# Layer A of a hybrid block: sums of weights packed four to a product, reciprocals sent round by DRAM, last rows in another order

## The chip, the cores and the metric

The kernel runs on one core of one Trainium2 chip. The metric is the time of one execution on the device, in microseconds. TensorE (PE) multiplies matrices into PSUM; VectorE (DVE), ScalarE (ACT) and GpSimd (POOL) work on tiles in SBUF, the first two on PSUM as well; SyncE (SP) issues nearly all DMAs.

## The reference

Four sequences of 2048 rows of 512 numbers go through four stages, each `x = x + f(layernorm(x))`: causal linear attention ("layer A"), a feed-forward product with both sides quantized to 8 bits, a gated recurrent attention ("layer B"), and the same feed-forward product again. The change lies in layer A and in the feed-forward product that directly follows it. Layer A is:

```python
q = relu(split_heads(x @ Wq)) + EPS          # 16 heads of 64
k = relu(split_heads(x @ Wk)) + EPS
v = split_heads(x @ Wv)
k_cumsum = cumsum(k, axis=2)                 # over the rows
context  = cumsum(einsum('bhnd,bhne->bhnde', k, v), axis=2)
D_inv = 1.0 / einsum('bhnd,bhnd->bhn', k_cumsum, q)
attn = einsum('bhnd,bhnde,bhn->bhne', q, context, D_inv)
return attn.reshape(b, n, H * DH) @ Wo + bo
```

`D_inv` is one number for each row and head: one over the sum of the weights with which earlier rows enter. The feed-forward product scales each row by its largest absolute value over 127, rounds it, does the same with the columns of `rhs`, multiplies and scales back.

## The kernel before

A flag computed from the decays chooses a code path at the start; with these inputs the "mild" one runs, `layer_a_mild` and then `layer_b_mild`. What follows is `layer_a_mild`.

The 8192 rows are cut into 16 blocks of `TA` = 512 rows. Tiles hold features on the 128 partitions and the 512 rows along the free axis, so that a pair of heads (2 x 64 features) fills the partitions; there are `NP` = 8 pairs. The main loop runs over blocks `n` and, within a block, over the pairs `hp`. One pass of the inner loop is called a slot here. In a slot `attend(B, hp)` gives six steps for one pair, and `fill` is a list of single products (one matmul each) of other work; `spread` puts the fill evenly between the six steps. The steps are

- `keys` (L815): `k` transposed on TensorE (`pkr`), copied by ScalarE to `kr`; VectorE makes the running sum of `k` within chunks of 128 rows (`qc`, a scan, L824), the carried sums (`ksum`), and multiplies by `q` (L831). `qc` has one buffer.
- `scores` (L836): eight products `pss`, masked by VectorE into `sm` (L849).
- `update` (L854): eight products `pu`, copied by ScalarE; GpSimd adds them up into `within`, the state at each chunk's start (L869).
- `weigh` (L874): the sums of weights. The product `pd` of `qc` with a matrix `same` of 128 x 128, ones in two diagonal blocks of 64, adds up the 64 features of each head and puts the sum on all 64 partitions of that head. ScalarE makes `guess` = exp(-ln(`pd`)), and VectorE `miss` = -`pd` x `guess`.
- `outputs` (L886): four products `pn` from the states and eight from `sm`. VectorE multiplies `pn` by `guess` (L906) and by 2 + `miss` (L910), one Newton step of the reciprocal, into `oT[hp]`, which has 12 buffers.
- an empty step.

The fill holds the `k` and `q` features of the next pair (`pk`, `pq`, four matmuls each), in the first four slots `values` for the second half of the heads (`pv`) and `project` for the previous block (`po`, eight matmuls over the eight `oT`), in the last four slots `values` of the next block and `pf`, the feed-forward product of a row group of the previous block. All matmuls of the helper `product` have the one line L647.

The feed-forward part for 128 rows: `ffn_levels` (L653) normalizes, finds the row's largest absolute value and rounds into `f_q`; `ffn_product` (L669) has SyncE transpose `f_q` by a DMA into `f_qT` (one buffer); `pf` is made a slot later, and VectorE and GpSimd put the result back into `xa` (L679, L680). When the last row group is in, the block is stored to DRAM as `mmid` (L966), from which layer B reads. After the last block the same loop runs once more with no attention in it: only `project`, `ffn_levels` and `pf` of that block.

`quantize_rhs` (L85) loads `rhs`, transposed, in one piece of 1 MB and quantizes it; it is called after the second slot of the first block.

PSUM is dealt out in banks: three for products (`mm`: `pk`, `pq`, `pv`, `po`, `pd`, `pf`), two for `pss`, one each for `pn`, `pu` and transposes. The framework that builds the program keeps the dependencies and may move an instruction past others on its engine, so the order on an engine is near the order of the text and not the same; every engine runs its own instructions in that order.

Of the kernel before, what the change touches and what calls it, by code (L numbers as in the profile page):

```python
# [13 lines left out]
ALU = mybir.AluOpType  # L14
# [31 lines left out]
def hybrid_block_kernel(ctx: ExitStack, tc: tile.TileContext, t: dict, out: bass.AP):  # L46
# [95 lines left out]
    def ffn(pool, bank, x, n):  # L142
# [4 lines left out]
        for i in range(n):  # L147
# [10 lines left out]
            qT = pool.tile([P, KC, P], BF16, name="f_qT", bufs=1)  # L158
# [494 lines left out]
    def ffn_levels(pool, x):  # L653

        mv, rs = stats(pool, x.unsqueeze(1), 1)
        sc = pool.tile([P, 2], F32, name="f_sc", bufs=4)
        xn = pool.tile([P, D], F32, name="f_xn", bufs=1)
        normalize(xn, x, mv, rs, 0)
        s1, v1 = sc[:, 0:1], sc[:, 1:2]
# [9 lines left out]
    def ffn_product(pool, bank, x, q, s1):  # L669

        qT = pool.tile([P, KC, P], BF16, name="f_qT", bufs=1)
# [10 lines left out]
        return [product]  # L682

    def layer_a_mild():
        with ExitStack() as es:
# [37 lines left out]
            same = w.tile([P, P], F32, name="same")  # L723
            nc.gpsimd.memset(same, 0.0)
            for h in range(2):
                nc.gpsimd.memset(same[h * DA : (h + 1) * DA, h * DA : (h + 1) * DA], 1.0)
# [77 lines left out]
            def attend(B, hp):  # L804
# [10 lines left out]
                def keys():  # L815
# [7 lines left out]
                    A.qc = pool.tile([P, TA], F32, name="qc", bufs=1)  # L823
                    nc.vector.tensor_tensor_scan(A.qc, go, k, 0.0, ALU.mult, ALU.add)  # L824
                    sums = ksum[:, hp, :]
                    ends = A.qc.rearrange("p (i t) -> p i t", t=P)[:, :, P - 1]
# [3 lines left out]
                    for i, ch in enumerate(chunks):  # L830
                        nc.vector.scalar_tensor_tensor(  # L831
                            A.qc[:, ch], A.qc[:, ch], sums[:, i : i + 1], q[:, ch], ALU.add, ALU.mult
                        )
# [40 lines left out]
                def weigh():  # L874

                    A.pd = bank([P, TA], F32, name="pd", tag="mm")
                    nc.tensor.matmul(A.pd, same, A.qc, start=True, stop=True)  # L877
                    ln = pool.tile([P, TA], F32, name="ln", bufs=1)
                    nc.scalar.activation(ln, A.pd, AF.Ln)
                    A.guess = pool.tile([P, TA], F32, name="guess", bufs=1)  # L880
                    nc.scalar.activation(A.guess, ln, AF.Exp, scale=-1.0)

                    A.miss = ln
                    nc.vector.scalar_tensor_tensor(A.miss, A.pd, -1.0, A.guess, ALU.mult, ALU.mult)

                def outputs():  # L886
# [15 lines left out]
                    for r in heads:  # L902
# [3 lines left out]
                    nc.vector.tensor_tensor(  # L906
                        A.guess, pn.rearrange("p i t -> p (i t)"), A.guess, ALU.mult
                    )
                    B.oT[hp] = pool.tile([P, TA], F32, name="oT", bufs=12)
                    nc.vector.scalar_tensor_tensor(B.oT[hp], A.miss, 2.0, A.guess, ALU.add, ALU.mult)  # L910
# [3 lines left out]
            def block(n, x):  # L914
                B = Block()
                B.n, B.x, B.xn, B.qk, B.v, B.oT, B.mul = n, x, {}, {}, {}, {}, {}
                return B

# [8 lines left out]
            for n in range(len(at) + 1):  # L927
                more = n + 1 < len(at)
                if n < len(at) and at[n][1] == 0:
# [4 lines left out]
                for hp in range(NP):  # L934
                    fill = []
                    if n < len(at):
                        if hp + 1 < NP:
                            fill += feature(B, hp + 1, "k") + feature(B, hp + 1, "q")
                        elif more:
                            fill += feature(after, 0, "k") + feature(after, 0, "q")  # L940
                        if hp < NTA:
                            fill += values(B, 1, hp)
                        elif more:
                            fill += values(after, 0, hp - NTA)
                    if prev is not None:
                        if hp < NTA:
                            fill += project(prev, hp)
                        else:
                            i = hp - NTA
                            fill = fill + prev.mul[i]  # L950
# [4 lines left out]
                    spread(attend(B, hp) if n < len(at) else [lambda: None], fill)  # L955
# [499 lines left out]
```

## Time and profile before

| | us |
|---|---|
| runs before: median (lowest to highest of 3) | 4247.15 (4246.32 to 4254.92) |
| the profiled execution | 4246.83 |
| its span, first to last instruction | 4244.9 |
| layer A, steady part (window 200 to 2540) | 2340 |
| last rows of layer A and start of layer B (window 2540 to 2625) | 85 |

What some of the groups of instructions cost in layer A, mean of one in ns (groups by line and shape, within 100 to 2540 us):

| line, engine, what | mean ns | count in the window |
|---|---|---|
| L824 DVE scan into `qc` | 1220 | 124 |
| L849 DVE mask into `sm` | 683 | 248 |
| L884 DVE `ln` (`miss`) from `pd` | 688 | 124 |
| L906 DVE `guess` from `pn` | 686 | 124 |
| L910 DVE `oT` | 770 | 124 |
| L879 ACT table load, then Ln | 1283, 598 | 125, 124 |
| L881 ACT table load, then Exp | 1283, 630 | 124, 124 |
| L822 ACT copy of `pkr` | 585 | 124 |
| L680, L748 POOL additions of 128 x 512 | 1267, 1268 | 59, 57 |

DMAs, from issue to landing (median): `mmid` 1 MB 4.3 us, `xa` 1 MB 5.1, `xb` 512 KB 3.7, the transposes into `f_qT` 2.4, `m_causal` 64 KB 2.0; rows of 2 KB spread over 128 partitions (256 KB each): `b_out_b` 4.8, `b_ln_g` 6.7, `b_ln_b` 7.8, `a_bo` 8.1.

In the timelines below a line is: start in us, time from its start to its end, engine, line, operation, output <- inputs, the part of the array used (rows * columns), shape and type, how many records were merged; in brackets, idle time before it and what ended it. A matmul of 32-bit floats leaves two records. Matmuls are pipelined, so what one costs is the time from its start to the next one's start.

### The profile page before, as it was taken

How to read it: one execution, taken by the hardware profiler on the slowest of the kernel's cores; microseconds unless marked ns; L12 is line 12 of the kernel's file. 1: busy time of each engine (PE TensorE's matmuls, PEld its weight loads, DVE VectorE, ACT ScalarE, POOL GpSimd, SP SyncE). 2: the span in 40 equal slices, each digit the busy share in tenths (PEclk: the TensorE clock that was granted, in tenths of full speed). 3: DMA queues.
4: the chain of work that ended last, by engine and by line, in shares of the span. 5: the costliest groups of instructions: out<-in, count | busy, mean ns of one | idle time of the engine just before them, and what ended most of it. 6: DMA issues, size and time to landing. Idle time of an engine off the chain costs nothing.

```text
span 4244.9 us, 55766 instructions
## 1 busy us (share of the span) xinstructions
PE 4154.5 (98%) x22421; PEld 2350.8 (55%) x22421; DVE 2320.8 (55%) x4451; ACT 1032.6 (24%) x1737; POOL 1392.8 (33%) x2527
## 2 busy tenths in 40 slices
PE   8999999999999999999999996999999999999997
PEld 4555555555555555555555554666666666666664
DVE  4455555555555555555555455566556656565655
ACT  2322322322322222222222230212111211121111
POOL 3222222222222222222222222444444444444443
PEclk9999999999999999999999998999999999999998
DMA  3000000000000000000000003011111111111100
GB/s 122 2 3 23 26 3 23 26 3 23 25 3 23 25 3 23 25 3 23 25 3 23 16 5 123 19 31 32 33 36 36 32 31 31 31 32 32 35 18 24
DMA packets 124829, 111.96 MB, mean 26 GB/s; under 512 B 73232, under 2 KB 86416, under 8 KB 124560
## 3 DMA queue, kind: packets, MB, share of 16 engines
q1 hardware_dynamic: 123440, 106.73, 8.2%
q8 instruction: 178, 2.92, 0.3%
q10 hardware_dynamic: 1120, 1.57, 0.1%
q14 instruction: 91, 0.75, 0.1%
HBM read 57.94 MB, written 33.55 MB: 22 GB/s over the span
## 4 chain that ended last, share of the span: by engine, by line
PE 93%; DVE 3%; POOL 2%; DMA 1%; issue 1%; ACT 0%; SPq 0%; POOLq 0%; DVEq 0%; ACTq 0%
PE pr L1109 11%; PE pk L647 11%; PE pv L647 11%; PE po L647 11%; PE pq L647 11%; PE pvb L647 5%; PE py L647 5%; PE pss L843 3%; PE pn L898 3%; PE pl L1142 3%; PE pn L892 3%; PE pd L877 3%; PE ps L1201 2%; PE pf L677 2%; PE pu L859 2%; PE pyT L1240 2%
## 5 line engine op out<-in xcount | busy, mean ns | idle before, releaser
L647 PE MATMUL pk<-xnTa,a_Wk 128*128 128x512 f32 x1024 | 510.2, 611 | 0.0
L647 PE MATMUL pq<-xnTa,a_Wq 128*128 128x512 f32 x1024 | 490.6, 601 | 0.0
L647 PE MATMUL pv<-a_Wv,xnTa 128*128 128x512 f32 x1024 | 478.8, 601 | 2.9 <-ACT xnTa L140 2.9
L647 PE MATMUL po<-a_Wo_sb,oT 128*128 128x512 f32 x1024 | 465.5, 598 | 0.0
L647 PEld LDWEIGHTS pv<-a_Wv,xnTa 128*128 128x128 f32 x1024 | 190.1, 191 | 229.7 <-issue 225.7
L647 PEld LDWEIGHTS po<-a_Wo_sb,oT 128*128 128x128 f32 x1024 | 189.7, 190 | 226.1 <-issue 220.2
L647 PEld LDWEIGHTS pq<-xnTa,a_Wq 128*128 128x128 f32 x1024 | 187.6, 190 | 210.7 <-issue 205.2
L125 POOL TENSOR_SCALAR rs<-mv 128x1 f32<-128x1 f32 x320 | 80.8, 253 | 610.5 <-DVE mv L124 610.0
L824 DVE TENSOR_TENSOR_SCAN qc<-go,kT 128x512 f32<-128x512 f32 x128 | 156.2, 1220 | 200.2 <-PE pd L877 200.2
L1109 PE MATMUL pr<-xnTb,m_kT_sb 128*128 128x256 f32 x1024 | 259.4, 392 | 0.0
L1109 PE MATMUL pr<-xnTb,m_qT_sb 128*128 128x256 f32 x1024 | 253.4, 391 | 0.0
L869 POOL TENSOR_TENSOR within<-state,u 64x64 f32<-64x64 f32 x256 | 80.8, 316 | 522.9 <-ACT u L864 513.3
L647 PE MATMUL pvb<-b_vT_sb,xnTb 128*128 128x512 f32 x512 | 246.9, 606 | 0.0
L849 DVE TENSOR_TENSOR sm<-pss,causal 128x512 f32<-128x512 f32 x256 | 164.3, 683 | 128.3 <-PE pss L843 127.1
L647 PE MATMUL py<-b_oT_sb,yT 128*128 128x512 f32 x512 | 231.5, 594 | 0.0
L647 PEld LDWEIGHTS pk<-xnTa,a_Wk 128*128 128x128 f32 x1024 | 169.0, 190 | 111.3 <-issue 92.8
L1109 PEld LDWEIGHTS pr<-xnTb,m_qT_sb 128*128 128x128 f32 x1024 | 185.4, 191 | 58.0 <-issue 25.9
L1109 PEld LDWEIGHTS pr<-xnTb,m_kT_sb 128*128 128x128 f32 x1024 | 184.5, 190 | 51.1 <-issue 19.9
L822 ACT COPY kr<-pkr 128x512 f32<-128x512 f32 x128 | 74.9, 586 | 557.5 <-PE pkr L820 557.5
L126 POOL TENSOR_TENSOR rs<-rs,neg_half 128x1 f32<-128x1 f32 x320 | 192.7, 603 | 23.3
L864 ACT COPY u<-pu 128x256 f32<-128x256 f32 x128 | 47.6, 372 | 620.1 <-PE pu L859 620.1
L793 DVE TENSOR_TENSOR xa<-po,xa 128x512 f32<-128x512 f32 x64 | 44.2, 691 | 263.3 <-PE po L647 263.3
(155 smaller groups left out, 6976.8 us busy)
## 6 DMA issues: line engine op xcount, KB each, us to landing
mmid<-xa SPq DMA_DIRECT2D x16, 1024.0 KB, 4.3
out<-xb SPq DMA_DIRECT2D x32, 512.0 KB, 2.8
xa<-in_x SPq DMA_DIRECT2D x15, 1024.0 KB, 5.1
xb<-mmid SPq DMA_DIRECT2D x30, 512.0 KB, 3.7
m_cos<-in_cos SPq DMA_DIRECT2D x30, 128.0 KB, 2.4
m_sin<-in_sin SPq DMA_DIRECT2D x30, 128.0 KB, 2.4
a_Wv<-in_a_Wv SPq DMA_DIRECT2D x2, 1024.0 KB, 7.6
a_Wk<-in_a_Wk SPq DMA_DIRECT2D x4, 512.0 KB, 9.6
```

The costliest lines, as they stand in the source:

```text
L126: nc.gpsimd.tensor_tensor(rs, rs, neg_half[:, :n], ALU.pow)
L647: nc.tensor.matmul(held[0], lhs(), rhs(), start=(n == 0), stop=(n == len(pairs) - 1))
L677: nc.tensor.matmul(pf, qT[:, c, :], rq[:, c, :], start=(c == 0), stop=(c == KC - 1))
L824: nc.vector.tensor_tensor_scan(A.qc, go, k, 0.0, ALU.mult, ALU.add)
L843: nc.tensor.matmul(ps[h][:, i, :], k[r, chunks[i]], q[r, chunks[i]], start=True, stop=True)
L849: nc.vector.tensor_tensor(s, ps[h], causal.unsqueeze(1).to_broadcast([P, NTA, P]), ALU.mult)
L859: nc.tensor.matmul(pu[r, i, :], A.kr[:, i, r], v()[:, i, vh[h]], start=True, stop=True, skip_group_check=True,)
L877: nc.tensor.matmul(A.pd, same, A.qc, start=True, stop=True)
L892: nc.tensor.matmul(pn[:, i, :], A.before[i], q[:, chunks[i]], start=(i == 0), stop=False, skip_group_check=True,)
L898: nc.tensor.matmul(pn[r, i, :], v()[:, i, vh[h]], A.sm[h][:, i, :], start=False, stop=True, skip_group_check=True,)
L1109: nc.tensor.matmul(pr[:, half, :], wp[name][:, c, lo : lo + P], B.xnT[:, c, :], start=(c == 0), stop=(c == KC - 1),)
L1142: nc.tensor.matmul(pl[half * 64 : (half + 1) * 64, n, :], low[name][:, f, g, half, :], B.turned[name][f][:, half, :], start=(f == 0), stop ...
```

## The change

1. `same` becomes 128 x 32: ones from the first 64 partitions to the first 16 columns, from the other 64 to the next 16. `weigh` does nothing in three slots of four. In slots 3 and 7 it makes four products, one for each of the last four pairs, each into a quarter of the 128 partitions of one bank `pd`. Each head's sum then stands on 16 partitions. `qc` gets four buffers.
2. Ln, Exp and the Newton step run once on that bank. Partition 0 of every 16 is written to DRAM (`rec`: 8 rows of 512 numbers) and loaded back, each row spread over the 64 partitions of its head, for two pairs at a time (`wide`, one buffer, two DMAs of 256 KB); after the last slot of the last block all four pairs at once, into the place of a tile `xnTa`.
3. `outputs` no longer divides: ScalarE copies `pn` to `oT`. Four `divide` steps per set multiply `oT` in place by `wide` on VectorE; they are put into the fill of the next slot at positions 6, 7, 13 and 15, and the second load follows the second of them.
4. The weights' quantization is split into four row groups, `load_part` and `quantize_part`, after the first five slots of the first block; `bo` is added row group by row group there. `f_qT` gets a second buffer.
5. The extra pass of the loop after the last block is gone. The first four products of the first two row groups of `project` are fill of the last slot; the rest of the last block is written out in an order of its own.

```diff
-            qT = pool.tile([P, KC, P], BF16, name="f_qT", bufs=1)
+            qT = pool.tile([P, KC, P], BF16, name="f_qT", bufs=2)
...
+    def load_part(pool, c):
+        rT = pool.tile([P, D], F32, name="f_xn", bufs=1)
+        nc.sync.dma_start(rT, t["rhsT"][c * P : (c + 1) * P, :])
+        return rT
+    def quantize_part(pool, bank, c, rT):
+        part = slice(c * P, (c + 1) * P)
+        q, s1 = row_levels(pool, rT)
+        transpose_rows(bank, rq[:, :, part], q, BF16)
+        wide = rT[:, 0:P]
+        nc.vector.tensor_copy(wide, s1.to_broadcast([P, P]))
+        pw = bank([P, P], F32, name="r_pw", tag="t")
+        nc.tensor.transpose(pw, wide, ident)
+        nc.scalar.copy(rscale[:, part], pw)
...
-            same = w.tile([P, P], F32, name="same")
+            same = w.tile([P, 32], F32, name="same")
             nc.gpsimd.memset(same, 0.0)
             for h in range(2):
-                nc.gpsimd.memset(same[h * DA : (h + 1) * DA, h * DA : (h + 1) * DA], 1.0)
+                nc.gpsimd.memset(same[h * DA : (h + 1) * DA, h * 16 : (h + 1) * 16], 1.0)
...
-                    A.qc = pool.tile([P, TA], F32, name="qc", bufs=1)
+                    qc = B.qc[hp] = pool.tile([P, TA], F32, name="qc", bufs=4)
...
                 def weigh():
-                    A.pd = bank([P, TA], F32, name="pd", tag="mm")
-                    nc.tensor.matmul(A.pd, same, A.qc, start=True, stop=True)
+                    if hp % 4 != 3:
+                        return
+                    pd = bank([P, TA], F32, name="pd", tag="mm")
+                    for m in range(4):
+                        nc.tensor.matmul(
+                            pd[m * 32 : (m + 1) * 32, :], same, B.qc[hp - 3 + m],
+                            start=True, stop=True, skip_group_check=True,
+                        )
                     ln = pool.tile([P, TA], F32, name="ln", bufs=1)
...
+                    nc.vector.scalar_tensor_tensor(ln, pd, -1.0, guess, ALU.mult, ALU.mult)
+                    nc.vector.scalar_tensor_tensor(guess, ln, 2.0, guess, ALU.add, ALU.mult)
+                    rec = dram.tile([4, 2, TA], F32, name=f"rec_{B.n}_{hp}")
+                    nc.sync.dma_start(rec.rearrange("m h t -> (m h) t"), guess[0:P:16, :])
+                    if B.n + 1 == len(at) and hp == NP - 1:
+                        wide = pool.tile([P, 4, TA], F32, name="xnTa")
+                        for h, r in enumerate(heads):
+                            nc.sync.dma_start(wide[r, :, :], rec[:, h, :].partition_broadcast(DA))
+                        wides = [wide[:, 0:2, :], wide[:, 2:4, :]]
+                    else:
+                        wides = [load(rec, 0)]
+                    def divide(m):
+                        o = B.oT[hp - 3 + m]
+                        nc.vector.tensor_tensor(o, o, wides[m // 2][:, m % 2, :], ALU.mult)
+                        if m == 1 and len(wides) == 1:
+                            wides.append(load(rec, 2))
+                    weights.extend([lambda m=m: divide(m) for m in range(4)])
+                def load(rec, m):
+                    wide = pool.tile([P, 2, TA], F32, name="wide", bufs=1)
+                    for h, r in enumerate(heads):
+                        nc.sync.dma_start(wide[r, :, :], rec[m : m + 2, h, :].partition_broadcast(DA))
+                    return wide
...
-                    nc.vector.tensor_tensor(
-                        A.guess, pn.rearrange("p i t -> p (i t)"), A.guess, ALU.mult
-                    )
                     B.oT[hp] = pool.tile([P, TA], F32, name="oT", bufs=12)
-                    nc.vector.scalar_tensor_tensor(B.oT[hp], A.miss, 2.0, A.guess, ALU.add, ALU.mult)
+                    nc.scalar.copy(B.oT[hp], pn.rearrange("p i t -> p (i t)"))
...
-            for n in range(len(at) + 1):
+            for n in range(len(at)):
...
+                    if not more and hp == NP - 1:
+                        row = [project(B, i) for i in range(NTA)]
+                        fill += row[0][:4] + row[1][:4]
...
+                    for place, f in zip((6, 7, 13, 15), weights):
+                        fill.insert(place, f)
+                    weights.clear()
+                    spread(attend(B, hp), fill)
+                    if n == 0:
+                        if 1 <= hp <= NTA:
+                            quantize_part(pool, bank, hp - 1, part)
+                            nc.gpsimd.tensor_tensor(B.x[:, hp - 1, :], B.x[:, hp - 1, :], bo, ALU.add)
+                        if hp < NTA:
+                            part = load_part(pool, hp)
...
+            run(row[2][:4])
+            run(weights)
+            run(row[0][4:])
+            levels(prev, 0)
+            run(row[1][4:])
+            levels(prev, 1)
+            run(row[2][4:] + row[3][:4] + prev.mul[0])
+            levels(prev, 2)
+            run(row[3][4:] + prev.mul[1])
+            levels(prev, 3)
+            run(prev.mul[2] + prev.mul[3])
+            store(prev)
```

`row_levels` is the second half of the former `ffn_levels`, from the largest absolute value on; `levels` calls `ffn_levels` and `ffn_product` for one row group, `store` writes `mmid`.

## The prediction

> **What bounds the kernel now.** I read the page first: busy shares, then the chain that ended last.
>
> ```profile
> PE 4154.5 (98%) x22421; PEld 2350.8 (55%) x22421; DVE 2320.8 (55%) x4451; ACT 1032.6 (24%) x1737; POOL 1392.8 (33%) x2527
> ...
> PE 93%; DVE 3%; POOL 2%; DMA 1%; issue 1%; ACT 0%; SPq 0%; POOLq 0%; DVEq 0%; ACTq 0%
> PE pr L1109 11%; PE pk L647 11%; PE pv L647 11%; PE po L647 11%; PE pq L647 11%; PE pvb L647 5%; PE py L647 5%; PE pss L843 3%; PE pn L898 3%; PE pl L1142 3%; PE pn L892 3%; PE pd L877 3%; PE ps L1201 2%; PE pf L677 2%; PE pu L859 2%; PE pyT L1240 2%
> ```
>
> TensorE is 93% of the chain, and `pd`, the product that the change packs, is 3% of it. Shares are averages, so next the windows: layer A in its steady state, and its last rows with the start of layer B.
>
> ```profile
> 200.00:2540.00 2340.00, 2339.38 (x11561) 1224.65 (x11560) 1232.42 (x2295) 657.25 (x881) 579.57 (x1413) 1.00 0.05 16
> 2540.00:2625.00 85.00, 52.13 (x178) 28.44 (x178) 43.38 (x144) 6.76 (x11) 25.22 (x37) 0.78 0.48 151
> ```
>
> After span and PE come PEld, DVE, ACT, POOL, clock, DMA. In 2340 us TensorE idles 0.6 us at full clock: there a matmul taken away is time taken away, until another engine is late. Vector is at 53%. In the last rows TensorE is 39% idle; there waits count.
>
> **Removed: 128 `pd` products.** A "busy" of 593 ns overlaps its neighbours; the cost is start to next start, from the timeline.
>
> ```profile
> 1005.64 1.02 PE L877 MATMUL pd<-qc,same 128*128 128x512 f32 x2
> 1006.50 1.88 PE L647 MATMUL pv<-a_Wv,xnTa 128*128 128x512 f32 x4
> 1008.22 1.02 PE L647 MATMUL po<-a_Wo_sb,oT 128*128 128x512 f32 x2
> ```
>
> One f32 product is two records, 0.86 us from 1005.64 to 1006.50 (0.43 each). 128 x 0.86 = 110.1 us.
>
> **Added: 32 sets of four, each a quarter of the columns.** If the quarters run one after another, nothing is gained (4 x 0.86). The nearest row is layer B's `pyT`: products of 32 columns, four quarters, a different moving operand each.
>
> ```profile
> 3009.61 0.64 PE L1240 MATMUL pyT<-ab,vb 128*32 128x128 f32 x16
> 3010.18 2.86 PE L1109 MATMUL pr<-xnTb,m_qT_sb 128*128 128x256 f32 x12
> ```
>
> Sixteen records of 128 columns; at 0.43/4 = 0.107 us each they would take 1.71 us one by one. They take 0.57: four rounds of four (0.43) plus 0.14. Cut to 3009.64 to 3009.68 the timeline shows four records begun together, and no more:
>
> ```profile
> 3009.61 0.32 PE L1240 MATMUL pyT<-ab,vb 128*32 128x128 f32 x4
> ```
>
> So a set of `pd` is 2 rounds x 0.43 + 0.14 = 1.00 us; 32 sets are 32.0. Net **-78.1 us**.
>
> Two rules of the Trainium skill speak against this. "TensorE: Matmul & The Clock Gate", Part 3, says that matmuls start and end in strict program order. Both passes of a product sit on one quarter; if the second waits for the first and the next quarter may not overtake, four quarters need five rounds, 5 x 0.43 + 0.14 = 2.29 us, and the net is 110.1 - 73.3 = 36.8. The same reading would give `pyT` nine rounds, 0.96 us, where the row has 0.57: I take the row. "TensorEngine Tiling", Key Properties, says that a change of tiling mode drains the array. `pd` was whole among whole products; now each set has a drain on each side. The pipeline's tail is what a record lasts beyond its spacing, 0.593 - 0.43 = 0.16 us; two would make 1.18 us a set, 6 us more in all. But `pyT` too stands beside whole products on both sides, so its 0.14 holds the drains; 1.00 stays, 1.18 is the bad end. The good end, no overhead, is 0.86: 4.5 us better.
>
> **Evictions.** Per pair Vector loses three passes (`ln` 0.69, `guess` 0.69, `oT` 0.77) and gains a multiply by the broadcast (SBUF only, like `oT`: 0.77); per set it gains two passes. 128 x 1.38 - 32 x 1.4 = 132 us less work. Scalar trades Ln, Exp and two table loads (0.60 + 0.63 + 2 x 1.28 = 3.8 us) for a copy of 0.59, and keeps the 3.8 once a set. Both hide under TensorE, so zero. `qc` with four buffers ends Vector's wait on `pd` (200 us in the rows); off the path, zero.
>
> **The round trip through DRAM is the new wait.** In the built order the first divide is queued on Vector right behind the second reciprocal pass; behind it wait the eviction of row 3's `po`, the FFN levels, and the next slot's masked scores, for which TensorE's `pn` waits. After `pd`: Ln 0.60, table 1.28, Exp 0.63, two passes 1.4, gaps and drain 0.3: 4.2 us. The write of 16 KB: no row of its own; 64 KB land in 2.0 (`m_causal`); with issue 2.4. Two broadcasts of 256 KB: the nearest rows, one row spread over 128 partitions, landed in 4.8 (`b_out_b`), 6.7 and 7.8 us (in a crowd of 11 loads), and 512 KB of `xb` in 3.7; I take 4.8 because little else moves here (DMA share 0.05), plus 0.6 issue. Sum 12.0 us after `pd`, between 10.5 and 15.
>
> Against it, fourth slot: `pd` ended at 1051.47 and the next slot began at 1063.03, 11.6 us later. So the data land 0.4 us into the next slot, two divides end at 2.0; before, Vector began the same work at 0.2 (1063.23) and finished the scores at 6.4 (1069.40). Delayed, they finish at 8.2. `pn` took them at 1074.75, 11.7 into the slot, 10.9 without `pd`. Slack 2.7 us: hidden. The second broadcast (issued at 2.0, landed by 7.4) is ready when Vector, done with the scores at 8.2, asks. Eighth slot: the rest of the slot after `pd` is 8.0 us, data at 4.0 into the next, divides to 5.5, the `kT` eviction and scan behind it to 7.7, scores by 9; `pn` needs them at 13.4. Slack 4.4. `oT` of the last pairs is wanted by `project` only after that. SP holds the write, the broadcasts, `mmid`, `xa` and the FFN transposes in one queue; in the built order a transpose waits up to a slot behind the second broadcast, but its product comes two slots later. Zero, up to 2.3 us a fourth slot (16 of them) at the 15 us end, 37 in all.
>
> **Slots without `pd`.** It also stood between `pu` and `pn`, which waits for GpSimd's `within`. In the last slot these were ready 3.5 us after `pu` began (2537.60 to 2541.14); without `pd` there remain `pu` 0.62 + four products 3.44 + 0.7 of `pn` = 4.8. Covered; where GpSimd first finishes an addition of 1.27 us, a little is not. +3 us over the layer (0 to 8); half of it is block 0, where this wait was already 1.24 us.
>
> **The quantized weights** come in four parts after slots 2 to 5 of block 0. The same 20 transposes; each part's load and Vector's 2 us sit beside slots that have no previous block to finish. Zero (-1 to +2).
>
> **The last rows.** Before, all 32 `po` products ran first (2543.5 to 2570.9), then `pf` waited for transposes one at a time, since `f_qT` had one buffer:
>
> ```profile
> 2570.93 1.03 PE L677 MATMUL pf<-rq,f_qT 128*128 128x512 bf16 x4
> 2574.33 1.04 PE L677 MATMUL pf<-rq,f_qT 128*128 128x512 bf16 x4 [2.38 <-DMA f_qT<-f_q]
> 2581.44 1.89 PE L677 MATMUL pf<-rq,f_qT 128*128 128x512 bf16 x4 [6.07 <-DMA f_qT<-f_q]
> 2588.18 1.89 PE L677 MATMUL pf<-rq,f_qT 128*128 128x512 bf16 x4 [4.86 <-DMA f_qT<-f_q]
> ```
>
> From the last `pd` (2538.91) to the issue of `mmid` (2592.30): 53.4 us. After, from `pd`: TensorE has 1.0 + two `po` 1.7 + `pn` 2.0 + seven `po` 6.0 = 10.7 us; the divided `oT` are back at 1.0 + 12.0 + 0.8 = 13.8, so it idles 3 us. Sixteen `po` bring 27.6. Row levels take Vector about 5 us each (2550.53 to 2555.80 shows one), rows overlap with each other's `po`, a transpose 2.5; in the built order the fourth levels end near 39.5, transpose 42, `pf` at half clock 1.9, `f_y` 0.75, addition 1.27: issue at 46. Gain 7.4, less 2.7 us of work that moved ahead of `pd`. Layer B's first loads follow `mmid` as before, with `b_oT` now among them: +1. Net -4 (-8 to +2).
>
> **Sum:** -78.1 + 3 - 4 = -79 us. Profiled execution 4246.8 (span 4244.9 and 1.9 around it), so 4167.8; the median of the runs, 4247.15, is 0.3 above it: **4168**.
>
> **Rivals.**
> - *The round trip costs part of the gain* (broadcasts of 7 to 8 us, as in the crowded rows): 3 us late, up to 0.7 us a fourth slot on TensorE, and Vector later still where it works near the slot's length; 10 to 30 us back, 4178 to 4198. For: partition broadcasts are the slow rows. Against: an idle DMA. 11%.
> - *Five rounds*: -36.8 + 3 - 4: 4209. For: the order rule. Against: `pyT`. 7%.
> - *Slower: Vector's queue at the first divide.* All behind it waits. With lateness x over my 12.0, a pair of sets loses (x - 2.7) + (x - 4.4) against a gain of 2 x 2.44 + 0.25 from the tail: even at x = 6.1, a landing of 10.9 us instead of 4.8. At 14 us (x = 9.2) a pair loses 11.3 against 5.1: 16 x 6.2 = 99, 4346. For: Vector is first in, first out, and the page has no read broadcast from freshly written DRAM. Against: no 256 KB row over 8.1. 5%.
> - *The quarters don't overlap at all*: two drains and no gain, near 4250. 1%; `pyT` excludes it.
>
> Forecast 76%. By itself it spans 4155 (no overhead, tail -8) to 4184 (drains, GpSimd at 8, tail +2). With most of the first rival: 4155 to 4193. A difference under 0.2% (8.5 us) can't be told from none here. Faster 0.94, same 0.01, slower 0.05.
>
> **What would show it.** `pd`: 256 records still, start to next start near 1.0 us a set (2.3: five rounds; 3.4: none overlap). TensorE idle in steady layer A under 8 us; a wait of `pn` for Vector's `sm` in the slot after a set is the DRAM rival, and the landing of `wide` says why. `mmid`'s last issue about 46 us after the last `pd`. Layer B unchanged. I am wrong if `wide` lands past 8 us or a set costs over 1.2.

## The result, and the profile after

| | median us (lowest to highest) | ratio to before, 95% interval |
|---|---|---|
| before, 4 runs beside the change | 4248.9 (4246.32 to 4254.92) | |
| after, 4 runs | 4199.38 (4198.64 to 4200.68) | 0.9882 [0.9865, 0.9899] |

The change makes the kernel 1.2% faster. I had forecast 4168 and a range of 4155 to 4193, so the direction was right and the gain too large by two thirds: the profiled execution (4199.37) has a span of 4197.5, 47.4 us below before, where my sum said 79. The page of the changed kernel, busy shares and chain:

```profile
PE 4100.3 (98%) x22421; PEld 2308.2 (55%) x22421; DVE 2200.0 (52%) x4271; ACT 749.0 (18%) x1484; POOL 1456.5 (35%) x2527
...
PE 91%; POOL 3%; DVE 3%; DMA 1%; issue 1%; ACT 0%; SPq 0%; ACTq 0%; POOLq 0%; DVEq 0%
```

and the windows of layer A's steady part and of its last rows with the start of layer B (columns as before):

```profile
200.00:2480.00 2280.00, 2276.81 (x11523) 1179.69 (x11522) 1114.33 (x2111) 391.45 (x640) 635.94 (x1407) 1.00 0.11 30
2480.00:2580.00 100.00, 64.75 (x237) 34.78 (x235) 54.60 (x160) 11.98 (x20) 34.62 (x50) 0.78 0.43 139
```

Vector and Scalar have the relief that was forecast, and TensorE is still what the steady part consists of. But it idles 3.2 us there where it idled 0.6, and its busy time over the whole kernel fell by 54 us (4154.5 to 4100.3), not by the 78 of the products that went. The last rows with the start of layer B are about as idle as they were, 35% (39% before). Where the 32 us are, read off as the times at which the same work begins in both traces (the start of `pkr` opens a slot; `pl`, `pvb` and `pke` are among the first products of layer B, in this order):

| stretch | my sum | measured |
|---|---|---|
| start to the first slot | 0 | +1.5 |
| block 1 | -4.9 + 1.5 | -0.2 |
| blocks 2 to 15 | 14 x -4.88 + 1.4 = -66.9 | -55.05 |
| block 16 up to its last slot | -4.9 | -2.7 |
| last slot to the issue of the last `mmid` | -4.6 | -0.2 |
| from there to layer B's first `pke` | +1 | +6.2 |
| rest of layer B, last stores | 0 | +3.0 |

(The +1.5 at the start is the scatter of the first loads: in the thirteen kernels below the first slot began 0.7 to 2.4 us earlier than in this one execution.)

**What came as forecast.** The quarters overlap. A set in the changed kernel, timeline of TensorE:

```profile
1026.76 1.98 PE L647 MATMUL pq<-xnTa,a_Wq 128*128 128x512 f32 x4
1028.58 1.02 PE L647 MATMUL pv<-a_Wv,xnTa 128*128 128x512 f32 x2
1029.54 1.06 PE L901 MATMUL pd<-qc,same 128*32 128x512 f32 x8
1030.53 2.84 PE L647 MATMUL pv<-a_Wv,xnTa 128*128 128x512 f32 x6
1033.21 1.02 PE L647 MATMUL po<-a_Wo_sb,oT 128*128 128x512 f32 x2
```

From 1029.54 to 1030.53 the set costs 0.996 us; I had 1.00. But look at its neighbours. Two records of `pv` before the set take 0.96 (1028.58 to 1029.54), and two whole records are 0.86; six behind it take 2.68 and are 2.58. The set is entered and left at 0.1 us each, and this stands in the rows of the products beside it. Summed over the 28 sets of blocks 2 to 15 the excess is 0.093 before and 0.104 behind a set, 5.5 us.

The round trip is hidden, as forecast: `wide` lands 4.0 us after issue (median of 124), and TensorE's list of waits has no `pn` waiting for Vector. It has three entries that my sum lacked or had too small (columns: who waited for what, us in total, times, longest):

```profile
PE pf L680 <- DMA f_qT<-f_q: 25.8, 5, 9.4
...
PE po L647 <- DVE oT L925: 4.1, 1, 4.1
PE pn L943 <- POOL within L889: 3.5, 10, 0.8
```

### The profile page after: what moved, and what is told of

Same layout as the page of the kernel before. It is cut to its first block, busy times and chain, and to the rows that moved or that the text cites. A ratio compares the mean times of both kernels' runs of the same rounds, so it can differ in the third digit from the quotient of the medians.

```text
span 4197.5 us, 55714 instructions
## 1 busy us (share of the span) xinstructions
PE 4100.3 (98%) x22421; PEld 2308.2 (55%) x22421; DVE 2200.0 (52%) x4271; ACT 749.0 (18%) x1484; POOL 1456.5 (35%) x2527
## 3 DMA queue, kind: packets, MB, share of 16 engines
q1 hardware_dynamic: 142400, 140.81, 11.3%
## 4 chain that ended last, share of the span: by engine, by line
PE 91%; POOL 3%; DVE 3%; DMA 1%; issue 1%; ACT 0%; SPq 0%; ACTq 0%; POOLq 0%; DVEq 0%
PE pr L1184 12%; PE pk L647 11%; PE pv L647 11%; PE po L647 11%; PE pq L647 10%; PE pvb L647 5%; PE py L647 5%; PE pss L863 3%; PE pn L949 3%; PE pl L1217 3%; PE pn L943 3%; PE ps L1276 2%; PE pf L680 2%; PE pu L879 2%; PE pyT L1315 2%; PE pg L647 2%
## 5 line engine op out<-in xcount | busy, mean ns | idle before, releaser
L889 POOL TENSOR_TENSOR within<-state,u 64x64 f32<-64x64 f32 x256 | 106.4, 416 | 546.7 <-ACT u L884 537.1
L889 POOL TENSOR_TENSOR within<-within,u 64x64 f32<-64x64 f32 x512 | 208.3, 407 | 38.3
L682 DVE SCALAR_TENSOR_TENSOR f_y<-pf,f_sc,rscale 128x512 f32<-128x512 f32 x128 | 94.6, 739 | 225.9 <-PE pf L680 200.4
```

Of the source, the lines that this page charges most:

```text
L682: nc.vector.scalar_tensor_tensor(y, pf, s1, rscale, ALU.mult, ALU.mult)
L889: nc.gpsimd.tensor_tensor(A.before[i + 1][r, r], A.before[i][r, r], u[r, i, :], ALU.add)
```

## The experiments

All are the changed kernel with one thing altered unless said otherwise; four runs each, beside seven of the kernel before on the same chip. The spans and slots are those of the profiled execution. In blocks 2 to 15 the slots repeat to 0.01 us from one kernel to the next where nothing touches them, so a difference of 0.1 us can be read, with one exception: the mean of the fifth slots, which follow a set, lies between 16.66 and 16.75 in the variants that leave them alone (16.67 in the changed kernel). A span also carries the scatter of the first loads, up to 2.4 us. The readings of the last rows rest on one trace for each kernel, and the runs of one kernel lie up to 10 us apart (those of the best version).

### Twice: is the overhead the set's, or the neighbours'?

```diff
-                    for m in range(4):
+                    for m in (0, 1, 2, 3, 0, 1, 2, 3):
```

> Every set of four pd products is issued twice in a row; the result is the same. Against the changed kernel. Theory (the cost that I missed is the change of tiling on the way into and out of a set, and it lies in the neighbours' spacing): a second set beside the first has no whole-array product between, so it adds only its 0.86 of columns: 32 x 0.86 = +27.5 us, and from the start of the doubled set to the start of the next product 0.996 + 0.86 = 1.86 us. Rival 1 (0.996 is the price of a set whatever stands beside it): +31.9 us, 1.99 us. Rival 2 (the whole 1.19 that a set took, with its neighbours, belongs to the set): +38 us, 2.19 us.

4228.51 us, ratio to before 0.9947 [0.9931, 0.9964]; span +30.3.

```profile
1038.62 1.02 PE L647 MATMUL pv<-a_Wv,xnTa 128*128 128x512 f32 x2
1039.57 1.92 PE L901 MATMUL pd<-qc,same 128*32 128x512 f32 x16
1041.43 2.84 PE L647 MATMUL pv<-a_Wv,xnTa 128*128 128x512 f32 x6
```

1039.57 to 1041.43 is 1.86: the second set added 0.86, its columns alone, and in every fourth and eighth slot of blocks 2 to 15. Of the span's other 2.8 us, 1.3 are fifth slots longer by 0.10, which is no more than they scatter; the rest lies in block 16, the last rows and the start of layer B, less 0.9 of the first loads. Both rivals fall: what a set has above its columns is paid once per stretch of tiled work.

### Beside `update`: is it the change of tiling?

```diff
-                return [keys, scores, update, weigh, outputs, lambda: None]
+                def both():
+                    update()
+                    weigh()
+
+                return [keys, scores, both, lambda: None, outputs, lambda: None]
```

> The set is issued straight behind update's pu products, which work in 64-column tiles, so that one stretch of tiled work less is entered and left: 7 changes of tiling in the fourth and eighth slot in place of 8. Against the changed kernel. Theory (each change costs about 0.1 us in the spacing): 32 x 0.1 = -3 us in the span, between -2 and -6, seen as fourth and eighth slots shorter by 0.1 to 0.2 us and no other slot moved. Rival (a set costs 1.19 wherever it stands): 0, within 0.5 us.

4189.11 us, 0.9856 [0.9839, 0.9872]; span -9.0, blocks 2 to 15 together -9.7: more than expected.

```profile
1021.21 0.69 PE L879 MATMUL pu<-va,kr 128*64 128x64 f32 x16
1021.82 1.06 PE L901 MATMUL pd<-qc,same 128*32 128x512 f32 x8
1022.82 1.98 PE L647 MATMUL pq<-xnTa,a_Wq 128*128 128x512 f32 x4
1024.64 3.60 PE L647 MATMUL pv<-a_Wv,xnTa 128*128 128x512 f32 x8
```

`pu` still costs 0.61, the set 1.00, and `pq` behind it 1.82, as it did behind `pu` alone in the changed kernel (1026.76 to 1028.58 above). The set rides in a stretch that is entered and left anyway. Fourth and eighth slots are shorter by 0.18 and 0.20: all that had stood in the neighbours' rows, 0.19 x 32 = 6.1 us. It is not the whole overhead: the set is still 0.14 above its columns (1.00 for 0.86), where a second set of the same tiling added its columns alone, so the step from 64 to 32 columns and the way out are still paid. The rest is a gain I had not expected: fifth slots are 0.32 shorter, 4.4 us over blocks 2 to 15, all of it in `pn`. The set is issued 2.8 us earlier, so the divisions fall a little earlier in the next slot, and GpSimd's `within` has a mean of 515 ns there in place of 565. What the one has to do with the other is the experiment after next.

### One piece: what the quantization in quarters costs

```diff
                         if 1 <= hp <= NTA:
-                            quantize_part(pool, bank, hp - 1, part)
                             nc.gpsimd.tensor_tensor(B.x[:, hp - 1, :], B.x[:, hp - 1, :], bo, ALU.add)
-                        if hp < NTA:
-                            part = load_part(pool, hp)
+                        if hp == 1:
+                            quantize_whole(pool, bank)
```

`quantize_whole` is the body of `quantize_rhs`, in tiles that stand free at that time.

> The weights rhsT are loaded and quantized in one piece behind the second slot of the first block, as before the change; the rest is the changed kernel. The first block then has 54 changes between whole-array and tiled products in place of 72. Theory (the quarters in slots 2 to 5 cost what the first block failed to gain, 4.3 us, through changes of tiling): the first block is shorter by 2 to 4.3 us (18 changes at 0.1 to 0.2), and so is the span. Rival 1 (quarters cost nothing, as I predicted; the first block lost its gain at the start of the program): within 0.5 us. Rival 2 (one piece waits for its 1 MB load and for Vector): longer by 1 us or more.

4197.42 us, 0.9876 [0.9859, 0.9892]; span -2.9, block 1 -2.8. It is chance that the two agree (the first slot began 1.3 us earlier, blocks 2 to 15 took 1.1 longer); the block is what I read. What the quarters do, changed kernel, around the start of slot 4 of block 1:

```profile
93.39 0.48 PE L863 MATMUL pss<-qT,kT 64*128 64x128 f32 x2
93.81 0.33 PE L701 MATMUL r_pw<-ident,f_xn 128*128 128x128 f32 x1
94.06 0.49 PE L863 MATMUL pss<-qT,kT 64*128 64x128 f32 x4
94.49 0.66 PE L840 MATMUL pkr<-ident,kT 128*128 128x128 f32 x4
...
```

and the same products with one piece:

```profile
95.20 1.16 PE L894 MATMUL pss<-qT,kT 64*128 64x128 f32 x16
96.29 1.98 PE L647 MATMUL pk<-xnTa,a_Wk 128*128 128x512 f32 x4
```

The sixteen `pss` cost 1.09 in one stretch. With `r_pw`, `pkr` and `pt` between them they stand in four, the first two of which cost 0.42 and 0.43 with six `pss`, and all four 2.07, beside what the whole products between them lose. Over block 1 `pss` took 2.65 us more than before the change, `pkr`, `pk`, `pq` and `r_pw` 1.9 more; one piece takes back 2.65 and 1.45, and loses 1.1 to a wait of `pn`. So the theory holds and so does a part of the second rival.

### No divisions: what GpSimd is slowed by

```diff
-                        nc.vector.tensor_tensor(o, o, wides[m // 2][:, m % 2, :], ALU.mult)
+                        nc.vector.tensor_tensor(o[:, 0:1], o[:, 0:1], wides[m // 2][:, m % 2, 0:1], ALU.mult)
```

Here 511 of 512 columns of `oT` are left undivided.

> The four divisions of a set work on one column in place of 512: the other 511 columns of oT are left undivided. Against the changed kernel. Theory[...]: within's mean in the fifth slot falls from 565 ns to 315 to 340 ns, the fifth slot is shorter by 0.38 us, 14 blocks by 5.3 us, and the last rows by the 2 us that the divisions take there: -6 to -8 us in all. Rival (the wait is one of order in GpSimd's queue[...]): within stays above 500 ns and blocks 2 to 15 stay the same within 1 us.

4188.53 us, 0.9856 [0.9839, 0.9872]; span -13.0, of which 1.8 are the scatter of the first loads. The fifth slot in the changed kernel, first GpSimd, then Vector at the same time:

```profile
1050.01 1.23 POOL L889 TENSOR_TENSOR within<-state,u 64x64 f32<-64x64 f32 x2 [3.38 <-ACT u L884]
1051.32 2.44 POOL L889 TENSOR_TENSOR within<-within,u 64x64 f32<-64x64 f32 x4
```
```profile
1049.66 1.41 DVE L925 TENSOR_TENSOR oT<-oT,wide 128x512 f32<-128x512 f32 x2
...
1051.92 1.34 DVE L844 TENSOR_TENSOR_SCAN qc<-go,kT 128x512 f32<-128x512 f32 x1
```

and GpSimd in that slot without the divisions:

```profile
1046.55 0.71 POOL L889 TENSOR_TENSOR within<-state,u 64x64 f32<-64x64 f32 x2 [3.65 <-ACT u L884]
1047.33 2.30 POOL L889 TENSOR_TENSOR within<-within,u 64x64 f32<-64x64 f32 x4
```

The two additions beside the divisions took 1.23 and take 0.71. The fifth slot is 0.37 shorter and blocks 2 to 15 are 5.23 shorter, all of it in `pn`: the number expected. The step on the way was off: `within` has a mean of 456 ns there, not 315 to 340, since additions beside the scan into `qc` are slow as well (the four at 1047.33). It stood at 337 in that slot before the change and stands at 565 after it. In block 16, whose slots are 13 us long, the fifth slot became longer, 14.16 us in place of 13.50: the scan, come forward, met additions there, and the six took 3.4 us in place of 2.8. A further 6.4 us lie behind the last slot, where I had expected 2. The last `po` came 7 us sooner behind the set and the last transposing load was issued 38.7 us behind it in place of 42.6, but that load now met layer B's weights and took 6.8 us to its product in place of 3.3, so the last `mmid` came only 0.5 sooner; layer B's first `pke` followed `mmid` by 52.5 us in place of 57.1. That asked for another theory of the last rows.

### The last rows and the start of layer B

Here each variant was aimed at one link, and each moved another. First the old order of the rows with the new packing (the loop's extra pass is back):

> The last block's rows are worked as before the change (one more pass of the slot loop, row after row, no product moved ahead of the set, the four divisions first); the packing and all else is the changed kernel. Theory (the new order of the rows is worth about what I put down, and the round trip through DRAM ate it): without it the round trip stands bare, and the store of mmid follows the set by 58 to 62 us in place of 50.05, less 3 us of products that run ahead there: span +5 to +9. My prediction's own step (new order worth 4 us in all): +4. Rival (the new order is worth nothing): within 1 us.

4198.49 us, 0.9873 [0.9857, 0.9890]; span -0.5: the new order of the last rows, to which my sum gave 4 us, is worth nothing, with the round trip in both.

Then the last set without DRAM (the reciprocals of the last four pairs spread by four products of 32 rows):

```diff
+                        def divide_here(m):
+                            o, part = B.oT[hp - 3 + m], slice(m * 32, (m + 1) * 32)
+                            ps = bank([P, TA], F32, name="ps", tag="s")
+                            nc.tensor.matmul(ps, made[0][part, :], guess[part, :], start=True, stop=True)
+                            nc.vector.tensor_tensor(o, o, ps, ALU.mult)
```

> The very last set of the layer does not go through DRAM: its reciprocals are spread to the 64 rows of each head by four more products (32 rows by 128 columns, made from a turned copy of the matrix same), and Vector divides by them out of PSUM. All else is the changed kernel. Theory (the round trip makes TensorE stand for 4.1 us and run at half clock behind it, which ate the 4 us that I had put down for the last rows): po goes on without the stand, row 0 is evicted 13 to 16 us behind the set in place of 20.7, and the store of mmid follows the set by 43 to 47 us in place of 50.05: -3 to -7. Rival (what ends the last rows is the chain of Vector, GpSimd and the transposing DMA of the last row, held up by the weight loads on the same queue, as without the divisions, where the products ended 7 us sooner and the store only 0.5): -0.5 or less.

4193.30 us, 0.9863 [0.9847, 0.9880]; span -5.7, of which 2.6 had come before the last slot began and are not its own. The stand of 4.1 us is gone (0.77 is left), but seven `po` (14 records) were put ahead of the new products, and the granted clock fell to 0.50 behind the new products all the same, from 2497.5 to 2500.9. The first row is evicted 19.97 behind the set (20.66 in the changed kernel), and `mmid` is issued 1.0 sooner, near the rival's side; `pke` follows it 2.4 sooner. The changed kernel's last rows, TensorE and SyncE, with two windows between them whose third number from the end is the granted clock (the share of full speed that TensorE was given):

```profile
2500.84 15.70 PE L647 MATMUL po<-a_Wo_sb,oT 128*128 128x512 f32 x32 [4.13 <-DVE oT L925]
...
2531.55 1.89 PE L680 MATMUL pf<-rq,f_qT 128*128 128x512 bf16 x4 [6.82 <-DMA f_qT<-f_q]
```
```profile
2497.60:2503.60 6.00, 2.76 (x4) 1.26 (x5) 2.50 (x4) 0.00 (x0) 0.00 (x0) 0.79 0.19 36
2503.60:2509.60 6.00, 6.00 (x14) 2.57 (x14) 2.16 (x5) 0.00 (x0) 0.79 (x2) 0.92 0.00 0
```
```profile
2522.48 0.58 SPq L82 DMA_DIRECT2D m_qT_sb<-in_m_qT  x1
2523.10 0.51 SPq L82 DMA_DIRECT2D m_kT_sb<-in_m_kT  x1
2528.21 1.20 SPq L675 DMA_TRANSPOSE f_qT<-f_q  x1
...
2535.66 0.38 SPq L973 DMA_DIRECT2D mmid<-xa  x1
2536.08 0.52 SPq L1087 DMA_DIRECT2D b_oT_sb<-in_b_oT  x1
...
2546.99 0.43 SPq L76 DMA_DIRECT2D b_out_b_row<-in_b_out_b  x1
```

Behind the stand the 32 records of `po` take 15.5 us, where 32 times 0.43 are 13.8; in finer windows the clock is 0.50 from 2502 to 2504 and 1.00 from 2505. The last row then waits for its transposing load, on a queue and on DMA engines that it shares with layer B's weights, 5 MB in all. In windows of 6 us the DMA engines have a busy share of 0.72 to 1.05 for 36 us from here on. And behind `mmid` (issued 2535.66) the small loads that layer B starts with wait until 2546.99, behind `b_oT`; before the change `b_out_b` was issued 4.4 us behind `mmid`, now 11.3. I tried to mend each.

`b_oT` from ScalarE's queue:

> Layer B's weights b_oT (1 MB) are loaded from ScalarE's queue; in the changed kernel they stand on SyncE's queue right behind the store of mmid and ahead of the small loads that layer B starts with. Theory (layer B lost some 6 us at its start because b_out_b waits behind that load, GpSimd waits for b_out_b, Vector's two normalizations wait for GpSimd, and Vector's chain of tables stands behind them): the chain of tables stands ahead of the normalizations again, the first pl follows the store of mmid by 31 to 33 us in place of 34.75, pl and pvb run at the full clock, the first pke follows by 50 to 53 us in place of 57.1, and the span is 4 to 6.5 us shorter. Rival 1 (the loss comes from TensorE's idling in the last rows and the clock behind it, not from the order of loads): within 1 us of the changed kernel. Rival 2 (ScalarE's queue now makes the loads of xb wait): longer.

4199.95 us, 0.9880 [0.9863, 0.9896]; span +1.6. `b_out_b` was issued 7.6 us behind `mmid` in place of 11.3, and `pke` followed `mmid` by 54.6 in place of 57.1; but the load now started 18 us ahead of `mmid` and met the third row's transposing load, 5.9 us from issue to its product where it had been 2.5. `mmid` came 4.6 later. A move of two things, which settles neither.

The first weights from ScalarE's queue, at the set:

> The changed kernel, with layer B's weights m_qT, m_kT, b_gT and low (3 MB) issued from ScalarE's queue, which is free behind the last slot; in the changed kernel they stand on SyncE's queue behind the transposing loads of the last rows. Theory, formed from the runs so far (the way from layer A's last rows into layer B is set by 7 MB of transfers, whose issue waits in SyncE's queue for the third row: from the issue of m_qT to the first pl there are 46 to 52 us in the changed kernel and the seven variants, whatever TensorE does before): 3 MB go while the engines of the DMA stand idle, the first pl follows the set by 73 to 78 us in place of 84.8, the span is 6 to 11 us shorter. Rival 1 (the chain of the last row through Vector and GpSimd sets the end): within 1 us. Rival 2 (the loads meet the round trip of the last set and make it later by as much): row 0 is evicted 3 to 5 us later than 20.7, the span gains less than 3.

4201.20 us, 0.9882 [0.9866, 0.9899]; span +2.8. The second rival, and more: the 2 MB met the round trip, TensorE stood 10.5 us for `oT` in place of 4.1, and `b_vT` and `b_oT` moved up and met the last row's load (7.8 us). My "46 to 52 us from the first weight to `pl`" held in the changed kernel and the variants up to then (it was 66.5 before the change) and broke in this one, with 84: it was no law.

`b_vT` and `b_oT` behind layer B's first rows:

```diff
-            nc.sync.dma_start(wv, t["b_vT"].rearrange("(c p) n -> p c n", p=P))
             out_b, ln_g, ln_b = (load_row(w, name) for name in ("b_out_b", "b_ln_g", "b_ln_b"))
-            nc.sync.dma_start(wo, t["b_oT"].rearrange("(c p) n -> p c n", p=P))
+            for m, name in ((wv, "b_vT"), (wo, "b_oT")):
+                nc.vector.tensor_copy(m[:, 0, 0:1], xs[0][:, 0, 0:1])
+                nc.sync.dma_start(m, t[name].rearrange("(c p) n -> p c n", p=P))
```

> The changed kernel, with layer B's weights b_vT and b_oT (1 MB each) loaded behind the first rows xb and behind the small loads (a copy of one column makes each load wait for xb). Theory (the 2 MB ahead of the small loads and of xb are what makes layer B late): the store of mmid follows the set by 50 us as before, b_out_b is issued 4 to 6 us behind it in place of 11.3, the first pl 29 to 31.5 us behind it in place of 34.75 and at the full clock, the first pke 49 to 51.5 in place of 57.1; the span is 5 to 8 us shorter. Rival 1 (TensorE's idling and its clock make the loss, not the loads): within 1 us. Rival 2 (b_vT now comes too late for pvb): pl sooner, pvb not.

4197.63 us, 0.9874 [0.9858, 0.9891]; span -1.9. What was to be told apart came out in part: `b_out_b` is issued 5.0 us behind `mmid`, `pl` follows it by 31.6, `pke` by 53.0, where 49 to 51.5 was expected and `pl` at full clock (it had 0.69). So the order of the loads makes 4 of the 6 us at the start of layer B. But `mmid` itself came 2.5 later: the first load of `xb` moved up in turn (2523.87 for 2531.11), ahead of the last transposing load, which took 4.9 us in place of 3.3. That the one made the other is not shown.

### All together

> All four mends together: the set beside pu, the weights quantized in one piece, b_oT on ScalarE's queue, the last set without DRAM. If they add up: -9.0 -2.9 (both measured) -5 -4 (both expected above) = -21 us against the changed kernel's span of 4197.5, 4173 to 4181. Rival (the ends of the layer are one chain, and the last two gain the same microseconds): 4182 to 4186.

4182.28 us, 0.9837 [0.9821, 0.9853]; span 4181.9: the set beside `pu` and the one piece kept their gains in the blocks; from the last slot to the last product only 1.0 us was won. The rival's case.

With the early weights in place of the late `b_oT`, the last set by DRAM and without:

> Set beside pu (-9.0 measured), weights quantized in one piece (-2.9 measured) and the early weights of the run before: 4197.5 - 12 - (6 to 11) = a span of 4174 to 4180 by the theory. Rival (early weights bring nothing): 4185 to 4187.

> As the run before, and the last set goes without DRAM, its divisions ahead of the third row's products, so that no transfer of layer A's stands among the weights. By the theory 2 to 5 us below the run before (the stand of 4.1 us is gone and row 0 comes 6 us sooner). Rival (the end is set by the transfers alone): the same within 1 us.

4186.29 us, 0.9851 [0.9835, 0.9868], span 4183.5; and **4177.94 us (4174.5 to 4184.4), 0.9832 [0.9816, 0.9849]**, span 4176.3. The first is the rival's case, 1.5 us better. The second is 7.2 below it, more than expected: without the round trip no transfer of layer A's stands among the early weights. This is the lowest median found, 21 us below the changed kernel, and faster than the kernels before and after the change.

With the late `b_vT` and `b_oT` besides:

> As e11 (set beside pu, weights quantized in one piece, early weights, last set without DRAM), with b_vT and b_oT loaded late as in the run before. Theory (the last row's transposing load met b_vT and b_oT, 5.8 us in e11): that load takes 3 to 3.5 us, the store of mmid follows the set by 51.5 to 52.2 us in place of 54.4, the first pke by 99 to 102 in place of 104.2; span 4170 to 4174. Rival (the transfers are one total that must pass before pl, whatever their order): within 1 us of e11's 4176.3.

4180.56 us, 0.9836 [0.9819, 0.9852]; span 4179.9, outside both expectations, though its runs (4177.9 to 4182.8) overlap with those of the version before it. The transposing load took 2.5 us in place of 5.8 and `mmid` came 3.3 sooner, as expected; `pke` came 2 us later all the same. The first `pl` of layer B in TensorE's timeline, in e11 and in this one:

```profile
2554.90 0.65 PE L1264 MATMUL pl<-xc_q,low_q 128*64 128x256 f32 x4 [1.62 <-issue]
```
```profile
2554.29 1.12 PE L1265 MATMUL pl<-xc_q,low_q 128*64 128x256 f32 x4 [3.31 <-issue]
```

TensorE stood 3.3 us ahead of `pl` in place of 1.6 and came back at half speed, 1.12 in place of 0.65 for the same four records, at a granted clock of 0.50 in place of 1.00.

## Why the prediction was right, and where it failed

- *The mechanism and its first term were right.* 128 products left at 0.858 us, 32 sets came at 0.996, the quarters overlap, the row `pyT` against my reading of the rule of program order was the right choice. The round trip costs nothing in the steady part. None of the rivals came about; that the measured time lies next to the range of the first (4178 to 4198) is chance, for no `pn` waited for Vector.
- *"`pyT` too stands beside whole products on both sides, so its 0.14 holds the drains; 1.00 stays"*: this step failed. The rule of the Trainium skill ("TensorEngine Tiling", Key Properties: a change of tiling mode drains the array) agrees with the trace, and I read the wrong rows to weigh it. The greater part of the price, 0.093 before and 0.104 behind a set, lies in the spacing of the whole products on both sides; only 0.14 lies in that of the tiled ones. It stood in the trace of before: the four whole `pyT` ahead of the quarters (line L1233) take 0.54 from start to start, where four `pt` of the same size among whole products take 0.44, and the twelve `pr` behind them take 2.69 where twelve are 2.59. The neighbours' rows and the set beside `update` show it: 0.19 to 0.20 us a set, 6.1 to 6.3 in all. My bad end, 1.18 a set, had the size, by luck: from the length of a record beyond its spacing.
- *"The quantized weights: zero (-1 to +2)"*: failed by the same mistake. I counted the transposes and not the places that they were put in. Eighteen more changes of tiling stand in the rows of block 1 with 4.1 us; one piece got 2.8 of it back.
- *"Slots without `pd`: +3"*: the wait was named right, its cause was not. I priced the missing cover of `pd`; in blocks 2 to 15 that costs nothing. What costs there is that the divisions, which work on SBUF alone, run beside GpSimd's additions and stretch them: 5.2 us. In block 16, whose slots are only 13 us long, slots 6 and 7 gained 0.34 where 0.86 was due, with and without divisions, and there it is the missing cover. The scan runs beside the fifth addition, which takes 1.12 us in the changed kernel and took 1.17 before it; `pd` had covered that wait, and now `pn` takes 1.50 in place of 0.98 (slot 6, GpSimd and TensorE):

```profile
2460.17 2.29 POOL L889 TENSOR_TENSOR within<-within,u 64x64 f32<-64x64 f32 x4
2462.51 0.49 PE L943 MATMUL pn<-qT,within 128*128 128x128 f32 x2 [0.25 <-POOL within L889]
```

- *"The last rows: net -4"*: failed; `mmid` was issued 50.05 us behind the set, not 46. 1.4 of that stood there when the set's first `oT` was back (15.2 for 13.8: the data landed 13.4 us after `pd`, not 12.0). 1.8 came from the sixteen `po` behind the stand, 15.5 us for 13.8: I had priced the stand and, for all but the last `pf`, put nothing for the lower clock behind it. 0.8 came from the last row's transposing load among layer B's weights, 3.3 for 2.5; the same load had taken 4.8 before the change, as the waits of 6.07 and 4.86 in my own lines could have told me. With 3 us of products moved ahead of the set nothing is left. The variants show that these terms do not add up: without divisions, and so without the stand, the last load was issued 3.9 us sooner and took 3.4 longer.
- *"Layer B's first loads follow `mmid` as before, with `b_oT` now among them: +1"*: the place was right, the size was not; +6.2. The 1 MB load ahead of eight small ones on one queue cost not its share of the bandwidth, but the time until the small ones are issued, and then the slower TensorE behind the longer wait. The late loads show 4 of the 6 us.
- *Open*: 2.4 us in blocks 2 to 15, 0.055 us in each of the slots 4, 6 and 7, where it lies in `pk` and in the `pt` that turn the next block's rows; 1.6 us late in layer B and 1.3 in its last stores. And no single change of the last rows was worth what its link showed, so I can name the links of that chain (transposing load, order of the loads, TensorE's speed after a stand) but not give each a price that adds up.

## What to carry to other kernels

Price a stretch of packed products by its columns plus what stands in its own row (0.14 us here) plus what stands in the rows of the whole products on both sides (0.2 us here); put it next to another tiled product, and the 0.2 falls away. When Vector's work changes from an operation that reads PSUM to one that reads only SBUF, look at what GpSimd does in those microseconds. Where two stages meet, list each queue's loads in order with their sizes, for a load moved out of one wait is found in the next, and a gain there is to be believed only from the start of the following stage.

## What the runs showed of the hardware that I had not expected

TensorE's speed after a stand. Idle time ahead of `pl` at the start of layer B, the time from `pl` to `pvb` (16 records of `pl`, the same in all), and the granted clock in that time:

| kernel | idle before `pl`, us | `pl` to `pvb`, us | granted clock |
|---|---|---|---|
| best version (e11) | 1.62 | 1.88 | 1.00 |
| no divisions | 1.74 | 1.88 | 1.00 |
| before | 1.91 | 1.87 | 1.00 |
| b_oT on ScalarE | 1.97 | 2.69 | 0.68 |
| late b_vT, b_oT | 2.21 | 3.05 | 0.69 |
| early weights | 2.34 | 3.40 | 0.54 |
| all together | 2.65 | 3.38 | 0.54 |
| early weights, set by DRAM (e10) | 2.82 | 3.19 | 0.58 |
| best version, late b_vT and b_oT (e13) | 3.31 | 3.61 | 0.50 |
| after | 4.40 | 3.61 | 0.50 |
| last set local | 5.48 | 3.61 | 0.50 |

In these kernels a stand of up to 1.9 us cost nothing, one of 3.3 us or more halved the clock of the next products, and in between the clock was halved for a part of them. So in the changed kernel 2.5 us more of waiting than before cost 1.7 us more behind it. These stands all follow some tens of microseconds of sparse work. The stand of 4.1 us ahead of `po`, behind dense work, was followed by a clock of 0.50 too, for 3.4 us. But the length of one stand does not decide alone: in the kernel with the last set local a stand of 0.77 us, behind products with gaps between them, was followed by 3.4 us at 0.50 as well.

Some of Vector's operations from SBUF to SBUF stretch GpSimd's additions (64 x 64 elements) beside them: 314 ns in slots where they stand alone, a mean of 565 in the slot that has divisions and the scan, 610 for the four at 1051.32, and up to 1.12 us for one beside the scan. Beside Vector's passes from PSUM into `qT` and `kT` alone they keep their 315 (176 of them in the changed kernel).
